# Seven 256-blocks for each 512x512 weight product, with group tiles and a new emission order

## The chip, the cores and the metric

The kernel runs on one core of a Trainium2 chip. The metric is device time in microseconds (us) of one launch. The engines are named as the profile names them: PE (TensorE, matmuls and transposes) with PEld (its weight loads), DVE (VectorE), ACT (ScalarE), POOL (GpSimd) and SP (SyncE, which issues most transfers). Each engine runs its own queue of instructions; semaphores join the queues. On PE an fp32 matmul leaves two records in the trace, each with its own weight load.

## The reference, cut to what matters

`x` is 128 x 128 x 512 (batch, node, feature) in fp32, `adj` is 128 x 128. Four layers follow one another, each with a residual and a layer norm over the 512 features:

```python
# layer 0: aggregate over nodes, then a 512x512 weight
x = _layernorm(x + (einsum('nm,bmd->bnd', adj, x) @ weight + bias))
# layer 1: scores of all pairs of nodes, masked by adj.T, scaled by their row norm, times values
q = einsum('bnd,ed->bne', x, Wq); k = einsum('bnd,ed->bne', x, Wk); v = einsum('bnd,ed->bne', x, Wv)
rel = adj.T * einsum('bnd,bmd->bnm', q, k)
x = _layernorm(x + einsum('bnm,bmd->bnd', rel / norm(rel, axis=2), v))
# layer 2: graph attention; h = x @ W; s1, s2 = h @ a1, h @ a2
att = softmax(leaky_relu(s1[:, :, None] + s2[:, None, :], 0.2) * adj, axis=2)
x = _layernorm(x + elu(att @ h + beta * h))
# layer 3: W1 = W2 = adj; the largest value over the features, then relu
A = einsum('od,bdn->bon', adj, x); C = A + b
x = _layernorm(x + max(relu(A[:, :, None, :] + (C - A)[:, :, :, None]), axis=-1))
```

## The kernel before, in words

The 128 batch elements are taken in 32 groups of four (`G = 4`, `NG = 32`). A tile of one element is 128 nodes (partitions) by 512 features. Every layer is a function that returns a list of steps for one group, and each step issues the instructions of one element or of the whole group.

**Layer 0** (`layer0`): `aggregate(b)` multiplies by `adjT` and leaves the transposed result in PSUM (p_y, L211); ACT copies it out as `yT` (L219); POOL adds the bias to `x` into `x1` (L208). `project(b)` multiplies `yT` by `w0_sb`, four matmuls of 128 x 512 (p_o, L224), and DVE adds `x1` out of PSUM (L227). `stats` (L165, L166) and `normalize` follow.

**Layer 1** (`layer1`): `turn(b)` transposes an element on PE (p_xT, L189), ACT copies it into `xT` (L190). `middle(c)` multiplies the group's `xT` by a 128-column part of `m_qk`, the product of Wq and Wk (p_t, L258), ACT copies it to `tT` (L265). `scores` gives p_rel (L271), DVE multiplies by `adj` (L279), POOL squares (L281), `norms` sums the squares on PE (p_n, L296) and a power on POOL gives the reciprocal norms. `values(b)` multiplies by `wvT` (p_v, L287; ACT copies, L291). `attend(b)` multiplies `rel` by the values (p_o, L304), DVE scales and adds the residual (L305).

**Layer 2** (`layer2`): `dots(b)` takes two products with `wa` on DVE (scr, L343, both inputs in SBUF, each with an accumulator). `logits` turns them on PE (p_s, L356), then DVE adds and takes the leaky relu (L362, L368), POOL multiplies by `adj` (L369), DVE finds the maximum (L371), ACT takes four exponentials (L374), DVE takes the reciprocal (L382) and scales (L384, with the beta term added). `turn_att` transposes the attention (p_eT, L392; ACT copies, L394), `gather(b)` multiplies `x2` by it (p_z, L399; ACT copies, L407), `project(b)` multiplies by `w2_sb` (p_h, L412). The elu is one exponential on ACT from PSUM (L416) and two operations on DVE (L417, L420).

**Layer 3** (`layer3`): `widen(b)` multiplies by `adjT` (p_a, L449), DVE finds the row maximum (L451) and adds the bias (L453), ACT adds it to the tile (L454); at the end four output transfers are issued from SP (L460).

`normalize` adds epsilon on DVE (L174), takes the power -0.5 on POOL (L169), and then makes four passes on DVE, one for each element: subtract the mean, multiply by the reciprocal deviation (L178).

So each group has four products with a 512 x 512 weight (lines L224, L258, L287, L412), of 16 matmuls (32 records) each. All tiles of an element are their own (`tiles(...)`, ten buffers for a tag), and PSUM is one pool of eight banks.

The order of the work is that in which the steps are called. Each step of layer `l` of group `g` has a place, and the steps are called in the order of their places:

```python
for g in range(NG):
    for l, layer in enumerate((layer0, layer1, layer2, layer3)):
        steps = layer(g)
        for i, f in enumerate(steps):
            pieces.append((g + 1.15 * l + (i + 0.5) / len(steps), l, f))
```

So in one unit of place layer 0 of a group, layer 1 of the group before, layer 2 of the one before that, and so on, are interleaved. Two pieces of set-up have places of their own: `prepare_weights` (`m_qk`, `wvT`) at 1.0 and `prepare_scores` (`wa`, eight DVE products in L120 and eight transposes) at 1.5. The framework derives the semaphores from the tiles, and sets the final order within each engine's queue itself.

## Time and profile before

| | |
|---|---|
| time, median of 3 runs (lowest, highest) | 2537.17 us (2536.48, 2537.85) |
| the profiled execution's own time | 2536.99 us |
| its span in the profile | 2535.2 us |
| matmuls of one 512x512 product | 1024 records, 458 to 461 us busy |
| matmuls of 128 columns: p_y, p_z, p_rel | 136.4, 138.0, 119.6 us busy |
| p_a and p_o of `attend` (512 columns) | 134.0 and 131.0 us busy |
| DVE: BATCH_NORM_STATS2 (L165) | 512 of 685 ns |
| DVE: norm passes (L178) | 512 of 540 ns, 243.9 us |
| DVE: addition out of PSUM (L227) | 128 of 683 ns |
| DVE: `dots` (L343) | 256 of 681 ns |
| ACT: copy out of PSUM (L265) | 128 of 586 ns |
| ACT: pass with a bias for each partition (L454) | 128 of 722 ns |
| POOL: bias addition (L208) | 128 of 1370 ns (median 1272) |
| POOL: power of 128x4 (L169) | 128 of 1043 ns |
| load of x for one group | 1024 KB, 5.7 us to landing |
| granted clock of PE, mean | 0.994 |

The busy time of an engine is the time in which at least one of its instructions ran; a mean duration on PE is longer than the distance between two matmuls, since they are pipelined, so distances are taken from the starts in the timeline. The span is cut in 40 slices in the page; PE is at nine tenths or more in all but the first and the last.

### The profile page before, as it was taken

To read this page: it belongs to the slowest core of one execution; us is meant where nothing else is said; L and a number is where in the kernel's file an instruction comes from. 1 tells how busy PE (TensorE), PEld (TensorE's weight loads), DVE (VectorE), ACT (ScalarE), POOL (GpSimd) and SP (SyncE) were. 2 spreads that over 40 slices of the span, in tenths; PEclk is the share of its full clock that TensorE was granted. 3 is DMA by queue.
4 is the path that set the end of the run, shared out by engine and by line. 5 is a ranking of instruction groups with operands and counts; after the bars stand their busy time and mean duration, and the time that the engine had idled before them with its cause. 6 is when DMAs were issued, how large, how long until landed. Compare 5 with 4: busy or idle time off the path is not lost.

```text
span 2535.2 us, 23625 instructions
## 1 busy us (share of the span) xinstructions
PE 2467.0 (97%) x8761; PEld 1338.9 (53%) x8761; DVE 1373.8 (54%) x3287; ACT 597.1 (24%) x1192; POOL 414.3 (16%) x358
## 2 busy tenths in 40 slices
PE   7999999999999999999999999999999999999994
PEld 4555555555555555555555555555555555555552
DVE  3354555554556655555645555545566455555466
ACT  1122222222222222222222222222222222222222
POOL 2111111111111111111211111111111111111011
PEclk9999999999999999999999999999999999999997
DMA  4000000000000000000000000000000000000001
GB/s 146 17 17 17 34 34 29 22 17 34 34 34 17 34 17 34 34 33 17 17 34 34 34 22 29 17 34 34 34 17 31 19 34 34 34 17 1 17 17 50
DMA packets 38802, 74.71 MB, mean 29 GB/s; under 512 B 2976, under 2 KB 3104, under 8 KB 38688
## 3 DMA queue, kind: packets, MB, share of 16 engines
q1 hardware_dynamic: 36960, 69.81, 7.5%
q10 hardware_dynamic: 1728, 3.41, 0.4%
q8 instruction: 69, 1.13, 0.2%
q14 instruction: 45, 0.37, 0.0%
HBM read 39.65 MB, written 33.55 MB: 29 GB/s over the span
## 4 chain that ended last, share of the span: by engine, by line
PE 96%; DVE 2%; ACT 2%; DMA 0%; POOL 0%; issue 0%; POOLq 0%; DVEq 0%; SPq 0%; ACTq 0%
PE p_t L258 18%; PE p_o L224 17%; PE p_v L287 17%; PE p_h L412 17%; PE p_z L399 5%; PE p_y L211 5%; PE p_rel L271 5%; PE p_o L304 4%; PE p_a L449 4%; PE p_xT L189 2%; ACT xT L190 1%; PE p_n L296 1%; PE p_eT L392 1%; PE p_m L142 1%; PE p_s L356 1%; DVE x L178 0%
## 5 line engine op out<-in xcount | busy, mean ns | idle before, releaser
L258 PE MATMUL p_t<-xT,m_qk 128*128 128x512 f32 x1024 | 458.2, 595 | 23.4 <-ACT xT L190 23.4
L224 PE MATMUL p_o<-w_sb,yT 128*128 128x512 f32 x1024 | 460.6, 593 | 0.0
L412 PE MATMUL p_h<-w_sb,zT 128*128 128x512 f32 x1024 | 460.6, 592 | 0.0
L287 PE MATMUL p_v<-wvT,xT 128*128 128x512 f32 x1024 | 460.5, 592 | 0.0
L227 DVE TENSOR_TENSOR x<-p_o,x 128x512 f32<-128x512 f32 x128 | 87.4, 683 | 558.3 <-PE p_o L224 558.3
L165 DVE BATCH_NORM_STATS2 st<-x 128x6 f32<-128x512 f32 x512 | 343.1, 685 | 34.6 <-ACT x L454 29.9
L258 PEld LDWEIGHTS p_t<-xT,m_qk 128*128 128x128 f32 x1024 | 189.5, 190 | 245.8 <-issue 214.5
L412 PEld LDWEIGHTS p_h<-w_sb,zT 128*128 128x128 f32 x1024 | 189.6, 190 | 214.3 <-issue 206.9
L178 DVE TENSOR_SCALAR x<-x,mv,rstd 128x512 f32<-128x512 f32 x512 | 243.9, 540 | 96.3 <-POOL rstd L169 96.3
L224 PEld LDWEIGHTS p_o<-w_sb,yT 128*128 128x128 f32 x1024 | 187.5, 191 | 199.5 <-issue 199.5
L287 PEld LDWEIGHTS p_v<-wvT,xT 128*128 128x128 f32 x1024 | 187.3, 190 | 199.4 <-issue 199.2
L208 POOL TENSOR_TENSOR x<-x,bias_sb 128x512 f32<-128x512 f32 x128 | 175.0, 1370 | 459.9 <-DVE x L305 440.5
L169 POOL TENSOR_TENSOR rstd<-ve,mhalf 128x4 f32<-128x4 f32 x128 | 132.5, 1043 | 633.5 <-DVE ve L174 621.2
L265 ACT COPY tT<-p_t 128x512 f32<-128x512 f32 x128 | 75.1, 586 | 499.3 <-PE p_t L258 499.3
L417 DVE SCALAR_TENSOR_TENSOR x<-p_h,x 128x512 f32<-128x512 f32 x128 | 88.0, 688 | 163.9 <-ACT m L416 163.9
L343 DVE SCALAR_TENSOR_TENSOR scr<-x,wa 128x512 f32<-128x512 f32 x256 | 174.4, 681 | 1.2
L211 PEld LDWEIGHTS p_y<-adjT,x 128*128 128x128 f32 x1024 | 135.6, 194 | 67.6 <-issue 67.3
L291 ACT COPY v<-p_v 128x512 f32<-128x512 f32 x128 | 74.3, 581 | 398.9 <-PE p_v L287 398.9
L399 PEld LDWEIGHTS p_z<-eT,x 128*128 128x128 f32 x1024 | 132.7, 193 | 46.5 <-issue 31.8
L416 ACT ACTIVATE m<-p_h 128x512 f32<-128x512 f32 x128 | 76.4, 597 | 330.2 <-PE p_h L412 327.3
L449 PE MATMUL p_a<-x,adjT 128*128 128x512 f32 x256 | 134.0, 608 | 14.1 <-DVE x L178 14.1
L211 PE MATMUL p_y<-adjT,x 128*128 128x128 f32 x1024 | 136.4, 277 | 8.0 <-DMA x<-in_x_dram 8.0
(62 smaller groups left out, 1979.8 us busy)
## 6 DMA issues: line engine op xcount, KB each, us to landing
x<-in_x_dram SPq DMA_DIRECT2D x32, 1024.0 KB, 5.7
out_dram<-x SPq DMA_DIRECT2D x128, 256.0 KB, 2.5
w_sb<-in_L_gnn_weight_dram ACTq DMA_DIRECT2D x1, 1024.0 KB, 5.9
wq_sb<-in_L_gnn_Wq_dram SPq DMA_DIRECT2D x1, 1024.0 KB, 16.1
wk_sb<-in_L_gnn_Wk_dram ACTq DMA_DIRECT2D x1, 1024.0 KB, 12.5
wv_sb<-in_L_gnn_Wv_dram SPq DMA_DIRECT2D x1, 1024.0 KB, 19.2
w_sb<-in_L_gnn_W_dram ACTq DMA_DIRECT2D x1, 1024.0 KB, 17.5
a_sb<-in_L_gnn_a_dram SPq DMA_DIRECT2D x1, 512.0 KB, 16.1
```

The source lines that it names most:

```text
L165: nc.vector.bn_stats(st, t)
L169: nc.gpsimd.tensor_tensor(r, v, mhalf, ALU.pow)
L178: nc.vector.tensor_scalar(ts[b], ts[b], mv[:, b, 0:1], r[:, b : b + 1], op0=ALU.subtract, op1=ALU.mult)
L208: nc.gpsimd.tensor_tensor(x1[g][b], xb, bias_sb, ALU.add)
L211: nc.tensor.matmul(p[:, k * P : (k + 1) * P], xb[:, k * P : (k + 1) * P], adjT, start=True, stop=True,)
L224: nc.tensor.matmul(p, yT[b][:, k, :], w0_sb[:, k, :], start=(k == 0), stop=(k == K - 1))
L258: nc.tensor.matmul(p, m_qk[:, k, c * P : (c + 1) * P], s["xT"][:, k, :, :].rearrange("p b n -> p (b n)"), start=(k == 0), stop=(k == K - 1),)
L287: nc.tensor.matmul(p, s["xT"][:, k, b, :], wvT[:, k, :], start=(k == 0), stop=(k == K - 1))
L343: nc.vector.scalar_tensor_tensor(scr, x2[g][b], 1.0, wa[:, i, :], op0=ALU.mult, op1=ALU.mult, accum_out=s["s"][:, i, b : b + 1],)
L399: nc.tensor.matmul(p[:, k * P : (k + 1) * P], x2[g][b][:, k * P : (k + 1) * P], s["eT"][:, b, :], start=True, stop=True,)
L412: nc.tensor.matmul(p, s["zT", b][:, k, :], w2_sb[:, k, :], start=(k == 0), stop=(k == K - 1))
L449: nc.tensor.matmul(p, adjT, x3[g][b], start=True, stop=True)
```

## The change

**The products.** The product of the group's 512 x 512 left factor (four elements of 128 nodes) with a 512 x 512 weight is cut into halves on both sides and formed from seven products of 256-blocks instead of eight (the Winograd form of Strassen's scheme). The weight sides (`weight_blocks`, four DVE operations for a weight) are made once, in set-up. The left sides are made for each product of each group (`left_factors`, four POOL operations). Each of the seven is four matmuls of 256 columns. Partial sums are kept in PSUM: blocks 1, 6, 7 and 4 add up in one region, 5 and 3 in a second one, 2 has a third; between the blocks the region's present state is taken out, by ACT as a copy where it is the first term of its quarter of the result, by DVE as an addition otherwise (in layer 0 always by DVE, onto `x1`).

```diff
+    ORDER = (1, 5, 2, 6, 3, 7, 4)
+    def left_factors(aT, tag, name, keep):
+        def blk(nh, kh):
+            return aT[:, 2 * kh : 2 * kh + 2, 2 * P * nh : 2 * P * (nh + 1)]
+        sums = work.tile([P, 3 + keep, 2, 2 * P], FP, tag=tag, name=f"s_{name}")
+        s1, s2, s4 = (sums[:, i] for i in range(3))
+        s3 = sums[:, 3] if keep else blk(1, 0)
+        nc.gpsimd.tensor_tensor(s1, blk(1, 0), blk(1, 1), ALU.add)
+        nc.gpsimd.tensor_tensor(s2, s1, blk(0, 0), ALU.subtract)
+        nc.gpsimd.tensor_tensor(s3, blk(0, 0), blk(1, 0), ALU.subtract)
+        nc.gpsimd.tensor_tensor(s4, blk(0, 1), s2, ALU.subtract)
+        return {1: blk(0, 0), 2: blk(0, 1), 3: s4, 4: blk(1, 1), 5: s1, 6: s2, 7: s3}
+    def by_rows(p, a, b, first):
+        for j in range(2):
+            for k in range(2):
+                nc.tensor.matmul(
+                    p[:, j, :],
+                    a[:, k, j * P : (j + 1) * P],
+                    b[:, k, :],
+                    start=(first and j == 0 and k == 0),
+                    stop=(j == 1 and k == 1),
+                    skip_group_check=True,
+                )
...
+        def put(dst, p):
+            if after is None:
+                nc.scalar.copy(dst, p)
+            else:
+                nc.vector.tensor_tensor(dst, p, dst, ALU.add)
+        def add(dst, p):
+            nc.vector.tensor_tensor(dst, p, dst, ALU.add)
+        def step(i):
+            a, b = factors()[i], weights()[i]
+            where = {1: 0, 6: 0, 7: 0, 4: 0, 2: 1, 5: 2, 3: 2}[i]
+            first = i in (1, 2, 5)
+            mul(region(where) if first else r[where], a, b, first)
+            p = r[where]
+            if i == 1:
+                put(c(0, 0), p)
+            elif i == 5:
+                put(c(1, 1), p)
+            elif i == 2:
+                add(c(0, 0), p)
+            elif i == 6:
+                put(c(0, 1), p)
+            elif i == 3:
+                add(c(0, 1), p)
+            elif i == 7:
+                add(c(1, 1), p)
+            else:
+                put(c(1, 0), p)
```

The weight sides:

```diff
+        t2, t3, t4 = t[:, 0], t[:, 1], t[:, 2]
+        nc.vector.tensor_tensor(t3, blk(1, 1), blk(0, 1), ALU.subtract)
+        nc.vector.tensor_tensor(t2, t3, blk(0, 0), ALU.add)
+        nc.vector.tensor_tensor(t4, blk(1, 0), t2, ALU.subtract)
+        nc.vector.tensor_tensor(blk(0, 1), blk(0, 1), blk(0, 0), ALU.subtract)
```

**Tiles and PSUM.** `x1`, `x2`, `x3`, the values and the layer-2 result are one tile for a group ([128, 4, 512]); `x` is loaded straight into `x1`, and POOL adds the bias in place after the aggregation has read it. PSUM is two pools of tags with four banks each: `ps` for single results, `r` for the regions of the products.

**The elu** is a step of its own (`elu(b)`): the layer-2 result is first copied or added into SBUF (`s["c"]`), and the exponential and the two DVE operations read it there.

**The norm passes** move to ACT, with one more small DVE operation for a group:

```diff
+        nm = small.tile([P, G], FP, tag="nmean", name=f"nmean_{key[0]}_{key[1]}")
+        nc.vector.scalar_tensor_tensor(nm, mv[:, :, 0], -1.0, r, op0=ALU.mult, op1=ALU.mult)
         for b in range(G):
-            nc.vector.tensor_scalar(
-                ts[b], ts[b], mv[:, b, 0:1], r[:, b : b + 1], op0=ALU.subtract, op1=ALU.mult
+            nc.scalar.activation(
+                t[:, b, :], t[:, b, :], AF.Identity, bias=nm[:, b : b + 1], scale=r[:, b : b + 1]
             )
```

**The order.** Each part of a layer is given a stretch of places of its own (`emit((from, to), *steps)`), with `t` = g - 1, g, g + 1 and g + 2 in layers 0, 1, 2 and 3, which follow one another here:

```diff
+        emit((t + 0.0, t + 0.2), *each(aggregate))
+        emit((t + 0.2, t + 0.21), sums)
+        emit(
+            (t + 0.25, t + 0.5),
+            *product(
+                f"y_{g}", by_rows, lambda: s["f"], lambda: bw["0"], rows_of(lambda: x1[g]), after
+            ),
+        )
+        emit((t + 0.5, t + 0.51), lambda: normalize((0, g), x1[g]))
...
+        emit((t - 0.2, t - 0.05), *each(turn))
+        emit((t - 0.05, t - 0.04), sums)
+        emit(
+            (t + 0.0, t + 0.25),
+            *product(
+                f"m_{g}", by_columns, lambda: s["f"], lambda: bw["m"], middle_block, None
+            ),
+        )
+        emit((t + 0.28, t + 0.46), *each(scores))
+        emit((t + 0.5, t + 0.51), norms)
+        emit(
+            (t + 0.5, t + 0.75),
+            *product(
+                f"v_{g}", by_rows, lambda: s["f"], lambda: bw["v"], rows_of(lambda: s["v"]), None
+            ),
+        )
+        emit((t + 0.76, t + 0.97), *each(attend))
+        emit((t + 0.98, t + 0.99), end)
...
+        emit((t + 0.0, t + 0.1), *each(dots))
+        emit((t + 0.1, t + 0.11), logits)
+        emit((t + 0.25, t + 0.26), turn_att)
+        emit((t + 0.29, t + 0.47), *each(gather))
+        emit((t + 0.5, t + 0.51), sums)
+        emit(
+            (t + 0.75, t + 1.0),
+            *product(
+                f"z_{g}", by_rows, lambda: s["f"], lambda: bw["2"], rows_of(lambda: s["c"]), None
+            ),
+        )
+        emit((t + 0.93, t + 1.05), *each(elu))
+        emit((t + 1.06, t + 1.07), end)
...
+        emit((t + 0.52, t + 0.74), *each(widen))
+        emit((t + 0.78, t + 0.79), end)
...
+    emit((-0.6, -0.59), prepare_qk)
+    emit((-0.1, -0.09), prepare_v)
+    emit((0.45, 0.46), prepare_scores)
```

In what follows Y, M, V and Z are the four products (layer 0, `m_qk`, values, layer 2), M5 is block 5 of M, and y0, at0, w0, xT0, elu0 are the steps of the group's first element; sumsY, sumsX and sumsZ are the left sides. M and V share sumsX. From one M to the next, the order of the places is: M1, y0, M5, y1, M2, `logits`, M6, y2, M3, y3, M7, sumsY, M4, `turn_att`, Y1, rel0, Y5, z0, Y2, rel1, z1, Y6, rel2, z2, Y3, rel3, Y7, z3, Y4, sumsZ, `norms`, norm of layer 0, V1, w0, V5, V2, w1, V6, w2, V3, V7, w3, V4, Z1, norm of layer 3, at0, Z5, xT0, at1, Z2, xT1, Z6, at2, xT2, Z3, xT3, at3, elu0, Z7, sumsX, elu1, Z4, norm of layer 1, elu2; dots0 to dots3, elu3 and the norm of layer 2 stand among M1 to M2.

## The prediction

> **What bounds the kernel now.** I read the page's busy shares first, then its chain of work that ended last, then the rows of the costliest lines, and last the timeline.
>
> ```profile
> PE 2467.0 (97%) x8761; PEld 1338.9 (53%) x8761; DVE 1373.8 (54%) x3287; ACT 597.1 (24%) x1192; POOL 414.3 (16%) x358
> ...
> PE 96%; DVE 2%; ACT 2%; DMA 0%; POOL 0%; issue 0%; POOLq 0%; DVEq 0%; SPq 0%; ACTq 0%
> ...
> L258 PE MATMUL p_t<-xT,m_qk 128*128 128x512 f32 x1024 | 458.2, 595 | 23.4 <-ACT xT L190 23.4
> L224 PE MATMUL p_o<-w_sb,yT 128*128 128x512 f32 x1024 | 460.6, 593 | 0.0
> ```
>
> TensorE is busy 97% and owns 96% of the chain: only less work on it, or less waiting, can shorten the span. Each fp32 matmul leaves two records, so a product of a group is 16 matmuls and 32 records. The timeline repeats every 77.03 us (the first `p_t` of two groups starts at 1263.44 and 1340.47), and 32 x 77.03 = 2465 of 2535.2 us; 70 us are start and end.
>
> ```profile
> 1209.30 1.05 PE L211 MATMUL p_y<-adjT,x 128*128 128x128 f32 x8
> 1210.19 3.74 PE L271 MATMUL p_rel<-tT,xT 128*128 128x128 f32 x32
> 1213.76 3.60 PE L287 MATMUL p_v<-wvT,xT 128*128 128x512 f32 x8
> 1217.20 0.60 PE L392 MATMUL p_eT<-ident,e 128*128 128x128 f32 x4
> ...
> 1261.67 1.04 PE L189 MATMUL p_xT<-ident,x 128*128 128x128 f32 x8
> 1263.44 3.70 PE L258 MATMUL p_t<-xT,m_qk 128*128 128x512 f32 x8 [0.73 <-ACT xT L190]
> ```
>
> From start to start: 32 records of 128 columns take 3.57 us (0.1116 each), 8 of 512 take 3.44 (0.430; 0.4294 over longer runs). The last row is a hand-over, TensorE to ScalarE and back: 0.59 us of copy cost 0.73 of idle after the matmul's modelled end, about 0.9 after its last column. It is the one wait of a group.
>
> **1. Work removed from TensorE.** A group's four products are 128 records of 0.4294 = 54.96 us. All else in the period is 77.03 - 0.73 - 54.96 = 21.34. Afterwards a product is 7 blocks of 8 records with 256 columns, 224 in all. No row has 256 columns: half a 512 gives 0.2147, two of 128 give 0.223; the straight line between both gives 0.217, which I take. 224 x 0.217 = 48.6 (48.1 to 50.0). A period without any wait is then **69.95 us**, 7.1 less.
>
> **2. Work added elsewhere, per group.** VectorE loses 16 norm passes (243.9/32 = 7.6 us) and gains 12 additions out of PSUM at 0.683 (8.2) and 4 small products (0.7): 43 us become 44. ScalarE gets the norm passes (16 x 0.72, by its nearest row, L454) and 4 copies: 18.7 become about 33. GpSimd gets 16 block sums at 1.27 (the adds of L208 and L369): 12.9 become 33. None of them fills 70 us; the question is when they are needed. The Trainium skill (ScalarE: Activation LUTs, section What ACT_TABLE_LOAD costs) adds some 93 ns for each pointer operand, and the new pass has two: about 0.8 us a pass, 1.3 us more a group on an engine half idle, which moves nothing. In set-up the four weights' block sums (16 adds of 0.68) run while inputs land or other set-up goes on.
>
> **3. New waits inside a product.** The order is 1, 5, 2, 6, 3, 7, 4, and 1, 6, 7, 4 add up in one PSUM region, each after the previous eviction. Step 4 comes directly after 7: eviction 0.68 plus hand-over, 0.9 to 1.1, less what is written between. In M nothing stands between (**1.1**); in Y a gather of 0.89 (**0.2**); in V a `widen` matmul of 0.86 (**0.4**); in Z only VectorE work (in step 4). Other reuses have two blocks or more between, 1.7 us and up, against an eviction of 0.6.
>
> **4. The wait that decides: `logits`.** TensorE runs as written. In the last group it waited 5.94 us for `e` though the `p_a` behind it was ready, and ran that only afterwards:
>
> ```profile
> 2484.01 0.48 PE L356 MATMUL p_s<-ident,s 128*128 128x128 f32 x1 [1.09 <-DVE scr L343]
> ...
> 2490.43 1.17 PE L392 MATMUL p_eT<-ident,e 128*128 128x128 f32 x4 [5.94 <-DVE e L384]
> 2491.39 1.92 PE L449 MATMUL p_a<-x,adjT 128*128 128x512 f32 x2
> ```
>
> VectorE, by contrast, takes what is ready: the set-up products of L120, written last, run ahead of the first evictions. The new places give, around a period's end, for TensorE: at3, Z7, Z4, M1, y0, M5, y1, M2, then the four transposes of `logits`, which need all `dots`. The `dots` need the layer-1 norm, which needs at3. From the end of at3 TensorE has 4 + 1 blocks at 1.74 and 2 x 0.89 (y): 5 x 1.74 + 1.78 = 10.5 us until it stands at `logits`. VectorE meanwhile has, back to back at 0.61 an operation: at3 1.4, the rest of elu0 1.3, Z7's eviction 0.6, elu1 1.9, elu2 1.9, elu3 1.9, eight `dots` 5.4, two norms' small steps 0.6, together **15.1**. In the order as written the layer-1 norm stood at 5.12 and `logits` at 5.58 of a group's count, 0.46 apart; now at 4.985 and 5.105, 0.12 apart, with one group's elu and two norms in the same stretch. Without any gap TensorE loses 15.1 + 0.4 - 10.5 = 5.0, Z4's wait included: the lower bound.
>
> It is raised by GpSimd. Its rows are the two-tensor adds of L208, VectorE's the two-tensor products of L120:
>
> ```profile
> 25.09 0.69 DVE L120 SCALAR_TENSOR_TENSOR scr_wa<-w_sb,a_sb 128x512 f32<-128x512 f32 x1
> 25.83 1.64 DVE L120 SCALAR_TENSOR_TENSOR scr_wa<-w_sb,a_sb 128x512 f32<-128x512 f32 x1
> 27.50 1.63 DVE L120 SCALAR_TENSOR_TENSOR scr_wa<-w_sb,a_sb 128x512 f32<-128x512 f32 x1
> ...
> 25.62 9.23 POOL L208 TENSOR_TENSOR x<-x,bias_sb 128x512 f32<-128x512 f32 x6 [8.32 <-DMA x<-in_x_dram]
> ```
>
> While GpSimd streams, the same product takes 1.64 instead of 0.69, about one slowed product for each add, and an add 1.54 instead of 1.23 (4.93 for the four at the start). In the 15 us at issue GpSimd now has sumsX (4 x 1.27), two norm powers (1.02) and two bias adds: 9.7 us, where VectorE has 15 operations with both inputs in SBUF (elu 7, dots 8; 9.2 us). Also, sumsX is written before the layer-1 norm, whose power queues behind it: the transposed copy ends 0.2 before at3 does, sumsX 5.1 to 6.7 after it, the power at 7.9, the mean at 8.3, the first pass on ScalarE at 9.2. Then follow at least eight dots (5.4), elu3 (1.9) and the rest of elu2 (1): 17.5, and with the bias adds in between about **19**. So 19 - 10.5 = **8.5** for Z4 and `logits` together. Counted another way, by the rows above: if half of the eight GpSimd operations meet a product, 15.5 + 4 x 0.95 = 19.3, so 8.8; if all do, 23.1, so 12.6, the upper bound. I stay at 8.5, nearer the middle, since the row shows the collision but not how often it falls here.
>
> The Trainium skill (SBUF — State Buffer, section Who interferes with whom) goes further than the row: a VectorE operation with two SBUF inputs and a GpSimd operation that reads SBUF exclude each other for the whole instruction, whatever their size. By it 9.7 + 9.2 = 18.9 us would have to pass one after the other, and the wait would be at least 8.4.
>
> **5. The granted clock.** After 5.08 us of idle, the eight `p_a` at 2518.20 (eight records) took 5.40 us where eight such records take 3.60. A wait of this length each group costs **1.8** more; none if it stays short (0.73 us cost nothing).
>
> **6. What is covered.** After `logits`, softmax takes 6.8 us to the end of L384 in the period shown (1206.0 to 1212.8); TensorE has 5 blocks and two aggregates, 10 us, before `turn`, so nothing; if GpSimd's y2, y3 adds delay it by over 3 us, the rest shows at `turn`. sumsY needs 5.1 us and its first result before Y5, some 7 us later. The 0.73 wait falls away, since block M1 reads only early columns. The x load moves nothing: three x1 buffers, one period of lead, 5.7 us of landing; output DMAs leave as before.
>
> **The sum.** Waits per period: 8.5 + 1.8 + 1.1 + 0.2 + 0.4 = 12.0. Ends: 70, plus an estimated 18, as the last group has no other group's matmuls over sumsZ (5.1), its three elu operations on two late tiles (4) and the longer dots chain (9): 88. 32 x 69.95 + 88 + 31 x 12.0 = 2238 + 88 + 372 = 2698 of span. The profiled run took 2536.99 with a span of 2535.2, so 1.8 on top: **2700 us**; that run lies 0.2 below the shown median, which moves nothing.
>
> **Rivals.**
> A. **VectorE keeps up** (faster). `logits` finds its dots done, or TensorE takes other matmuls first. For it: VectorE is idle 40% of a period. Against: the 5.94 us above. With 3 us of waits: 2326 + 93 + 2 = 2421.
> B. **No collisions with GpSimd.** Waits 5.0 + 1.0 + 0.2 + 0.2 = 6.4, no slow clock: 2326 + 198 + 2 = 2526, almost the old time; what the products save the waits take. For it: in steady state the rows of L343 stay at 669 to 694 ns. Against: GpSimd had 13 us a group there, not 33. It turns from gain to loss at 6.75 us of waits.
> C. **Worse blocking.** An order on VectorE that sets a norm's step, which waits for GpSimd, ahead of ready work. For it: 0.89 us of VectorE idle before the norm at 2479.61, with a `dots` product still to come. Against: it fills other gaps. The upper bound of step 4 with the clock's 1.8 and 2.6 for the products: 12.6 + 1.8 + 2.6 = 17.0, 2326 + 527 + 2 = 2855.
> D. **256-column matmuls not at half price**: at 0.223 each the main sum rises by 45, to 2745. Within the range.
>
> **Chances.** Forecast (2580 to 2800, D within it) 0.52; A 0.20; B 0.17; C 0.11. A measurement can tell about 0.2% (5 us) from no change. Faster: A and half of B, 0.28; same 0.03; slower 0.69. The range reaches down to 2430, which keeps B and the upper part of A, and up to 2820; about 0.2 is left out. The forecast's own range is 2580 to 2800.
>
> **What would show it.** Records of 256 columns 0.217 apart; `p_s` idle before it of 4 to 8 us in each group, released by `scr`; Z's and M's step 4 each waiting for VectorE; dots with mean over 0.9 us; TensorE's clock below 0.99 in the middle slices. Wrong would be: TensorE still at 97%, idle before `p_s` under 1 us, or `dots` at 0.68.

## The result, and the profile after

The changed kernel takes **2743.08 us** (median of four runs, 2735.86 to 2756.68) against 2537.09 us for the kernel before: 1.0818 times as long (95% interval 1.0776 to 1.0861). The prediction was 2700 us, 43 less; the measured time lies inside its range of 2430 to 2820 and inside the forecast's own range of 2580 to 2800. The profiled run is the shortest of the four, 2735.86 us with a span of 2734.1.

The page of the changed kernel, busy times and the chain that ended last by engine:

```profile
PE 2415.9 (88%) x11833; PEld 1984.9 (73%) x11833; DVE 1599.0 (58%) x3299; ACT 1021.5 (37%) x1836; POOL 923.2 (34%) x742
...
PEclk8999999999999999999999999999999999999997
...
PE 45%; POOL 20%; DVE 16%; ACT 14%; issue 4%; DMA 1%; ACTq 0%; POOLq 0%; DVEq 0%
```

TensorE's share fell from 97 to 88%, and it owns 45% of the chain instead of 96%: the end is now set by work that passes between four engines. GpSimd, at 34% busy, has the second largest share of the chain. Its 384 additional instructions (742 instead of 358) are twelve block sums a group; the prediction had counted sixteen.

TensorE's waits by releaser: us in all, times, longest:

```profile
PE p_s L474 <- ACT m L538: 92.1, 30, 3.1
PE p_eT L510 <- DVE e L502: 76.3, 62, 5.9
PE p_s L474 <- DVE scr L461: 45.8, 39, 5.8
PE r_v L212 <- DVE v L250: 30.8, 29, 1.1
PE r_z L212 <- DVE c L250: 14.4, 32, 2.1
```

The first row and the third are one wait, that of the transposes of `logits` for the `dots`. An exponential of the elu ended at about the time of the first wait's end, so the view names it; the product that the transpose reads (a `scr` row) ended at 1360.80 + 0.08, just ahead of the matmul at 1361.03.

One period in TensorE's timeline (start, duration, and in brackets the idle time before and what ended it):

```profile
1350.71 1.99 PE L212 MATMUL r_z<-t,zT 128*128 128x256 f32 x8 [0.37 <-DVE c L250]
...
1361.03 0.45 PE L474 MATMUL p_s<-ident,s 128*128 128x128 f32 x1 [3.09 <-ACT m L538]
1361.27 3.47 PE L225 MATMUL r_m<-s_x,t_m 128*128 128x256 f32 x8
...
1368.93 0.32 PE L474 MATMUL p_s<-ident,s 128*128 128x128 f32 x1 [0.90 <-DVE scr L461]
...
1376.96 0.33 PE L510 MATMUL p_eT<-ident,e 128*128 128x128 f32 x1 [1.40 <-DVE e L502]
1378.23 0.73 PE L510 MATMUL p_eT<-ident,e 128*128 128x128 f32 x2 [0.94 <-DVE e L502]
...
1396.06 0.83 PE L404 MATMUL p_n<-ones,sq 128*128 128x1 f32 x6 [0.36 <-POOL sq L398]
1414.03 1.99 PE L212 MATMUL r_v<-t_v,xT 128*128 128x256 f32 x8 [1.06 <-DVE v L250]
```

The `p_s` after the first wait returns at 1444.00, so this period is **82.97 us** (77.03 before); 28 of them, from 207.93 to 2531.79, have a mean of 83.0. Its idle stretches add up to 0.37 + 3.09 + 0.90 + 1.40 + 0.94 + 0.36 + 1.06 = 8.12, within 0.02 of the period less TensorE's busy 74.83 in it. The block of M behind the long wait takes 3.31 us to the next start where a block takes 1.73. The granted clock shows both places; windows of 5 us, with each engine's busy time and, after POOL's, the clock:

```profile
1361.03:1366.00 4.97, 4.97 (x20) 4.28 (x21) 4.91 (x16) 1.28 (x4) 0.17 (x1) 0.66 0.00 0
1366.00:1371.00 5.00, 4.10 (x24) 3.53 (x23) 2.89 (x7) 3.06 (x5) 3.29 (x3) 1.00 0.00 0
...
1376.00:1381.00 5.00, 3.10 (x13) 2.83 (x14) 3.30 (x5) 0.58 (x1) 2.03 (x2) 0.71 0.00 0
```

0.34 of 4.97 us and 0.29 of 5.00 are 3.1 us lost to the clock, and 0.3 more in the next window, with 0.95: 3.4 us. (The window from 1441.00 to the next long wait's end shows 0.82, but TensorE is idle in it, so nothing is lost there.) So 69.95 (TensorE's work as predicted) + 8.1 + 3.4 = 81.5. Idle times understate the rest: a block's modelled end lies 0.16 us behind the start of its successor, and seven such places give 1.1. The last 0.4 us are not traced.

What made `p_s` late is the chain of the changed kernel (start, us, what), from the last transposed copy of x to that transpose:

```profile
1346.07 0.59 ACT xT L370
1346.66 0.07 issue
1346.73 1.53 POOL s_x L202
1348.25 1.68 POOL s_x L204
1349.93 1.24 POOL s_x L203
...
1351.24 1.59 POOL s_x L205
...
1352.93 1.40 POOL rstd L291
...
1354.36 1.24 DVE nmean L300
...
1355.62 0.81 ACT x L302
```

Four block sums of x for the next product stand on GpSimd ahead of the power that the layer-1 norm of another group needs. VectorE's small operations of the norm are slow as well: `ve` (the variance plus epsilon, which the power reads) ran 1.23 us from 1351.63, beside the last sum, and the mean 1.24 us, beside a bias addition, both at 128 x 4 elements. The sums end at 1352.83 and `ve` at 1352.86, so the power was held up by both.

### The profile page after: what moved, and what is told of

The parts are those of the page before. It is cut to its first block, busy times and chain, and to the rows that moved or that the text cites. A ratio compares the mean times of both kernels' runs of the same rounds, so it can differ in the third digit from the quotient of the medians.

```text
span 2734.1 us, 30874 instructions
## 1 busy us (share of the span) xinstructions
PE 2415.9 (88%) x11833; PEld 1984.9 (73%) x11833; DVE 1599.0 (58%) x3299; ACT 1021.5 (37%) x1836; POOL 923.2 (34%) x742
## 4 chain that ended last, share of the span: by engine, by line
PE 45%; POOL 20%; DVE 16%; ACT 14%; issue 4%; DMA 1%; ACTq 0%; POOLq 0%; DVEq 0%
PE r_y L212 10%; PE r_z L212 10%; ACT x L302 6%; PE p_rel L386 5%; PE p_z L519 4%; PE r_m L225 4%; POOL rstd L291 4%; PE r_v L212 3%; PE p_o L415 3%; DVE st L287 3%; ACT x L576 2%; PE p_xT L367 2%; ACT e L492 2%; POOL s_x L204 2%; DVE nmean L300 2%
## 5 line engine op out<-in xcount | busy, mean ns | idle before, releaser
L302 ACT ACTIVATE x<-x,nmean,rstd 128x512 f32<-128x512 f32 x512 | 381.5, 805 | 355.0 <-DVE nmean L300 355.0
L247 DVE TENSOR_TENSOR x<-r_y,x 128x512 f32<-128x512 f32 x128 | 88.0, 688 | 285.2 <-PE r_y L212 285.2
L526 ACT COPY zT<-p_z 128x512 f32<-128x512 f32 x128 | 74.9, 585 | 421.3 <-PE p_z L519 421.3
L416 DVE SCALAR_TENSOR_TENSOR x<-p_o,rn,x 128x512 f32<-128x512 f32 x128 | 95.9, 749 | 132.5 <-PE p_o L415 132.5
L225 PE MATMUL r_m<-s_x,t_m 128*128 128x256 f32 x512 | 165.1, 480 | 0.0
L576 ACT ACTIVATE x<-x,top 128x512 f32<-128x512 f32 x128 | 91.8, 718 | 169.9 <-DVE top L575 168.3
L386 PE MATMUL p_rel<-tT,xT 128*128 128x128 f32 x1024 | 153.5, 293 | 0.0
L386 PEld LDWEIGHTS p_rel<-tT,xT 128*128 128x128 f32 x1024 | 149.4, 210 | 4.9
L250 DVE TENSOR_TENSOR x<-r_y,x 128x512 f32<-128x512 f32 x96 | 65.2, 680 | 146.3 <-PE r_y L212 146.3
L212 PE MATMUL r_y<-w_sb,s_y 128*128 128x256 f32 x512 | 143.6, 419 | 2.0 <-POOL s_y L202 2.0
L519 PE MATMUL p_z<-eT,x 128*128 128x128 f32 x1024 | 137.6, 279 | 0.7 <-ACT eT L512 0.7
```

Of the source, the lines that this page charges most:

```text
L212: nc.tensor.matmul(p[:, j, :], a[:, k, j * P : (j + 1) * P], b[:, k, :], start=(first and j == 0 and k == 0), stop=(j == 1 and k == 1), sk ...
L225: nc.tensor.matmul(p[:, c, :], b[:, k, c * P : (c + 1) * P], a[:, k, :], start=(first and c == 0 and k == 0), stop=(c == 1 and k == 1), sk ...
L302: nc.scalar.activation(t[:, b, :], t[:, b, :], AF.Identity, bias=nm[:, b : b + 1], scale=r[:, b : b + 1])
L386: nc.tensor.matmul(p[:, b * P : (b + 1) * P], s["xT"][:, k, b * P : (b + 1) * P], s["tT"][:, k, b * P : (b + 1) * P], start=(k == 0), stop ...
L519: nc.tensor.matmul(p[:, k * P : (k + 1) * P], x2[g][:, b, k * P : (k + 1) * P], s["eT"][:, b, :], start=True, stop=True,)
L576: nc.scalar.activation(x, x, AF.Identity, bias=top)
```

## The experiments

The kernel before took 2537.1 to 2537.7 us beside each of these. Where one value is given, it is of a single run. "The changed kernel" is put at its profiled 2735.9, the run that the traces describe.

**1. No block sums.** The left factors are plain blocks, so the result of every weight product is another one.

```diff
-        nc.gpsimd.tensor_tensor(s1, blk(1, 0), blk(1, 1), ALU.add)
...
-        return {1: blk(0, 0), 2: blk(0, 1), 3: s4, 4: blk(1, 1), 5: s1, 6: s2, 7: s3}
+        return {1: blk(0, 0), 2: blk(0, 1), 3: blk(0, 1), 4: blk(1, 1), 5: blk(1, 0), 6: blk(1, 1), 7: blk(1, 0)}
```

> Leaves out the 16 left-side block sums of a group on GpSimd: each of the seven blocks reads a plain block of the left factor, so the products are not the reference's; matmuls, evictions and order stay. Theory S (the stretch: TensorE waits at logits and turn because elu, dots and norms follow one another on VectorE, lengthened by collisions with GpSimd's sums, and each long wait lowers the clock): the waits at p_s and p_eT fall from 6.4 us a group to 2 to 3, e at L502 goes back to about 350 ns, and the period from 83 us to 75 to 78, so 2490 to 2590 us. Rival P (the blocks themselves: PSUM regions taken out between dependent blocks, 256-column matmuls): no change, 2720 to 2760. Rival N (the norm passes on ScalarE): no change beyond 1%.

Measured: **2529.0 us**. The sums cost 207 us, though TensorE does exactly the same matmuls. (GpSimd loses 12 sums a group, not 16.) The first line of its page and TensorE's waits in this run, by its own line numbers:

```profile
PE 2328.9 (92%) x11833; PEld 1929.5 (76%) x11833; DVE 1477.7 (58%) x3299; ACT 1024.6 (41%) x1836; POOL 441.4 (17%) x358
```

```profile
PE p_s L467 <- DVE scr L454: 113.4, 96, 5.8
PE p_eT L503 <- DVE e L495: 16.8, 21, 5.9
...
PE r_v L205 <- DVE v L243: 7.1, 29, 0.2
```

TensorE is idle 198 us instead of 318: 60 less at `p_eT`, 24 less at `p_s`, 24 less at V's block 4. The other 87 us are the same matmuls in less time (2328.9 busy instead of 2415.9), at a mean granted clock of 0.984 instead of 0.953. The two waits that theory S names come to 4.1 us a group, not the 2 to 3 that it gave: most of the wait at `p_s` stays without the sums.

**2. Logits later.**

```diff
-        emit((t + 0.1, t + 0.11), logits)
-        emit((t + 0.25, t + 0.26), turn_att)
-        emit((t + 0.29, t + 0.47), *each(gather))
-        emit((t + 0.5, t + 0.51), sums)
+        emit((t + 0.27, t + 0.28), logits)
+        emit((t + 0.47, t + 0.48), turn_att)
+        emit((t + 0.5, t + 0.66), *each(gather))
+        emit((t + 0.68, t + 0.69), sums)
```

> Order only: logits from place 0.10 to 0.27, turn_att from 0.25 to 0.47, gather from 0.29-0.47 to 0.50-0.66, sumsZ from 0.50 to 0.68. Theory S: the waits at p_s and p_eT and the slow clock after them go; the period becomes 71.5 to 75 us, 2380 to 2490 us, below the kernel before. Rival P: 2700 to 2750, since no product changes. Rival N: little, 2680 to 2750, as the norm passes stay on ScalarE.

Measured: **2594.8 us**. The `p_s` wait is almost gone (11.6 us), but the gain is too small by over 100 us, because a new wait stands in its place. TensorE's waits and its timeline in this run:

```profile
PE r_m L225 <- DVE tT L250: 142.4, 29, 4.9
...
PE p_s L474 <- DVE scr L461: 11.6, 6, 4.7
```

```profile
1306.57 3.78 PE L225 MATMUL r_m<-xT,t_m 128*128 128x256 f32 x8 [4.91 <-DVE tT L250]
1310.14 1.13 PE L212 MATMUL r_y<-w_sb,yT 128*128 128x256 f32 x3
```

M's block 4 writes into a region that VectorE must first read after block 7, and that addition is queued behind the dots. The slow block behind the wait is there again, 3.57 us.

**3. Norm passes back on VectorE.**

```diff
-            nc.scalar.activation(
-                t[:, b, :], t[:, b, :], AF.Identity, bias=nm[:, b : b + 1], scale=r[:, b : b + 1]
-            )
+            nc.vector.tensor_scalar(
+                t[:, b, :], t[:, b, :], mv[:, b, 0:1], r[:, b : b + 1], op0=ALU.subtract, op1=ALU.mult
+            )
```

> Undoes one part: the four norm passes of each layer go back to VectorE (540 ns each, 8.6 us a group). Theory S: VectorE gets more work in the very stretch, 2740 to 2830 us. Rival N: the chain of each norm gets shorter by ScalarE's 805 ns passes and its queue, 2600 to 2700 us. Rival P: no change.

Measured: **2837.0 us**, just above theory S's range, with 302.5 us of `p_s` waits. So this part of the change helps, by about 100 us.

**4. Plain products in the new arrangement.** Sixteen matmuls of 512 columns and four evictions for each product, no block sums; tiles, order, elu and norm passes as changed.

```diff
+        def step(i):
+            a, w = factors(), weights()
+            p = psum.tile([P, D], FP, tag="r", name=f"r{i}_{name}")
+            for k in range(K):
+                if mul is by_rows:
+                    nc.tensor.matmul(
+                        p, a[:, k, i * P : (i + 1) * P], w[:, k, :], start=(k == 0), stop=(k == K - 1)
+                    )
...
-        return [lambda i=i: step(i) for i in ORDER]
+        return [lambda i=i: step(i) for i in range(G)]
```

> Keeps the new tiles, order, elu and norm passes, but makes each product as before, 16 matmuls of 512 columns with four evictions, without block sums. TensorE then has 76.3 us of work a group. Theory S: no GpSimd sums, but the stretch stays: 2 to 4 us of waits a group at p_s and p_eT, 2570 to 2660 us, slower than the kernel before although its products are the same. Rival P: the loss lies in the blocks, so 2500 to 2550. Rival N: 2570 and more, with waits for ScalarE's norm pass.

Measured: **2624.5 us**, `p_s` waiting 87.4. The arrangement alone (order, tiles, elu and norm passes together; which of them, this run doesn't show) costs 87 us; the seven blocks with their sums then add 111 more in it, where TensorE has 7.1 us a group less to do.

**5. Another order of the blocks**, with a block between 6 and 7 and one between 7 and 4. Here the first element's elu reads the layer-2 result before block 3 is added.

```diff
-    ORDER = (1, 5, 2, 6, 3, 7, 4)
+    ORDER = (1, 5, 6, 2, 7, 3, 4)
```

> One size of the products alone: the blocks in the order 1, 5, 6, 2, 7, 3, 4, so that one other block stands between any two that use the same PSUM region. Theory S: of the 13 us that a group loses, only the waits at step 4 (r_v 1.0, r_z 0.5) go, and what TensorE arrives earlier it waits longer at p_s: 2690 to 2735 us. Rival P: the reuse of the regions is the loss, 2450 to 2600.

Measured: **2717.9 us**, 18 us less, which is within the 21 us over which the four runs of the changed kernel spread. V's block 4 no longer waits for VectorE, but `p_eT` waits 107.5 us instead of 76.3. So the waits inside the products are a small part at most.

**6 and 7. Everything of layer 2 later, with the old and the new order of blocks** (the latter with the elu as in the fifth). The tile of the values is allocated in `scores` instead of `norms` here, since `norms` now comes after V's first block.

```diff
-        emit((t + 0.0, t + 0.1), *each(dots))
-        emit((t + 0.1, t + 0.11), logits)
-        emit((t + 0.25, t + 0.26), turn_att)
-        emit((t + 0.29, t + 0.47), *each(gather))
-        emit((t + 0.5, t + 0.51), sums)
+        emit((t + 0.18, t + 0.42), *each(dots))
+        emit((t + 0.46, t + 0.47), logits)
+        emit((t + 0.62, t + 0.63), turn_att)
+        emit((t + 0.63, t + 0.74), *each(gather))
+        emit((t + 0.745, t + 0.75), sums)
...
-        emit((t + 0.5, t + 0.51), norms)
+        emit((t + 0.56, t + 0.57), norms)
```

> Order only, wider than late_logits: dots from 0.00-0.10 to 0.18-0.42, logits to 0.46, turn_att to 0.62, gather to 0.63-0.74, sumsZ to 0.745, norms from 0.50 to 0.56; blocks in the order of the change. late_logits left one wait of 4.9 us, M4 for M7's addition, which stands on VectorE behind the dots. Theory S: with the dots out of the way that wait falls under 1.5 us, the clock stays at 0.98 or more, the period is 71.5 to 74 us, 2370 to 2460 us. If instead the wait only moves to the next consumer of VectorE's work, 2500 to 2590.

> Both: the places of spread and the block order 1, 5, 6, 2, 7, 3, 4. Theory S: on top of spread the waits at step 4 (0.4 to 1 us in each of M, V and Z) go: 1 to 2.5 us less a group, 2330 to 2420 us, and the period within 2 us of the 69.95 that TensorE's work alone takes.

Measured: **2631.6** and **2602.1 us**. Both missed all that was stated. In the sixth, M's block 4 waits for VectorE 161 us in all, 5.5 at most. In the seventh, the wait goes to ScalarE; its timeline, and TensorE's below it:

```profile
1371.22 2.93 ACT L302 ACTIVATE x<-x,nmean,rstd 128x512 f32<-128x512 f32 x4 [3.53 <-DVE nmean L300]
1374.05 0.61 ACT L538 ACTIVATE m<-c 128x512 f32<-128x512 f32 x1
1374.57 0.56 ACT L245 COPY tT<-r_m 128x512 f32<-128x512 f32 x1
```

```profile
1375.28 1.96 PE L225 MATMUL r_m<-s_x,t_m 128*128 128x256 f32 x8 [2.97 <-ACT tT L245]
```

The copy out of M's region stands behind four norm passes in ScalarE's queue, and ScalarE was idle 3.53 us for their mean. That both misses have one cause, places set by what `logits` needs while the late norm stayed where it was, is argued here; the ninth and tenth test it.

**8. GpSimd as busy, reading nothing.** Each block sum becomes a sum of four columns and three memsets, so the left factors are others.

```diff
+        def fill(dst, a, b):
+            nc.gpsimd.tensor_tensor(dst[:, :, :4], a[:, :, :4], b[:, :, :4], ALU.add)
+            for _ in range(3):
+                nc.gpsimd.memset(dst, 0.5)
```

> Each of the four block sums on GpSimd is replaced by a sum of 4 columns (so that it still waits for its inputs) and three fills of the whole block with a constant, which read nothing; the left factors are then not the reference's. GpSimd is busy about as long as before. Theory C (collisions: two-input VectorE operations and GpSimd instructions that read SBUF get in each other's way): e at L502 goes back to 350 ns, and the time falls most of the way to that of no_sums, 2530 to 2620. Theory Q (the queue on GpSimd alone, the norm's power behind the sums): the time stays within 2680 to 2760.

Measured: **2696.9 us**, GpSimd busy 1080 us (923 in the changed kernel). VectorE's softmax operation (L502 of the changed kernel) takes 348 ns again instead of 808, and the waits at `p_eT` fall from 76 to 47 us; `p_s` still waits 155. So the slowing of VectorE beside GpSimd's sums accounts for at least some 40 of the 207 us; the rest stays as long as GpSimd is occupied in the same places, which points to its queue. The split is rough: GpSimd is 17% busier here, and TensorE's wait for it at `p_n` rises from 11 to 43 us.

**9. Sums of x earlier.** Only the place of x's transposes and sums changes.

```diff
-        emit((t - 0.2, t - 0.05), *each(turn))
-        emit((t - 0.05, t - 0.04), sums)
+        emit((t - 0.24, t - 0.13), *each(turn))
+        emit((t - 0.125, t - 0.12), sums)
```

> Only the order changes: the transposes of x and GpSimd's sums of x are issued earlier (transposes from -0.24 to -0.13 of a group's place instead of -0.2 to -0.05, the sums at -0.125 instead of -0.05), so that the four sums run before the layer-1 norm's small operations instead of beside them. Theory L (the late end of the layer-1 norm makes the dots late and so the logits' transposes wait; in the changed kernel the sums of x stood at 1346.73 to 1352.8 us, ve took 1.23 us beside them and the power came at 1352.93): the norm ends 2 to 3 us earlier and the p_s wait falls from 4.3 us per group to about 2: 2640 to 2700 us. Rival B (the dots end late because VectorE works through eight of them with the ELU's operations between, whatever the norm does): p_s keeps its 4 us, 2720 to 2755 us.

Measured: **2639.5 us** (two runs; 1.0403 of before, 1.0373 to 1.0433), 96 us below the changed kernel. The time is at the edge of what theory L said, but its row is not: `p_s` waits 133.8 us in all, hardly less. Counted from the start of the last residual addition of layer 1 (L416), the mean now comes after 5.6 us instead of 7.3 and the last dot ends after 20.1 instead of 21.8. What fell is another wait, `p_eT` with 36.5 instead of 76.3 us, and the time that the same matmuls take: TensorE is busy 2365.0 us instead of 2415.9, at a mean granted clock of 0.972 instead of 0.953. The wait at `p_s` is in three pieces (1.28, 0.64 and 2.20 us). In one group of three the block behind the last piece isn't slow, in the other two it takes 2.4 to 3.4 us to the next start instead of 1.73; two groups that follow one another:

```profile
1334.79 0.32 PE L474 MATMUL p_s<-ident,s 128*128 128x128 f32 x1 [2.20 <-DVE scr L461]
1334.95 1.89 PE L225 MATMUL r_m<-s_x,t_m 128*128 128x256 f32 x8
...
1414.24 0.32 PE L474 MATMUL p_s<-ident,s 128*128 128x128 f32 x1 [2.20 <-DVE scr L461]
1414.40 2.92 PE L225 MATMUL r_m<-s_x,t_m 128*128 128x256 f32 x8
```

VectorE's timeline in this run shows what is left:

```profile
1332.90 1.22 DVE L300 SCALAR_TENSOR_TENSOR nmean<-mv,rstd 128x4 f32<-128x4 f32 x1 [0.90 <-POOL rstd L291]
1334.05 0.68 DVE L461 SCALAR_TENSOR_TENSOR scr<-x,wa 128x512 f32<-128x512 f32 x1
```

The mean of another norm (layer 2's) stands ahead of the last dot, waits 0.90 us for GpSimd, and takes 1.22 us beside a bias addition.

**10. Early sums and later logits together**: the edit of the ninth, and

```diff
-        emit((t + 0.1, t + 0.11), logits)
-        emit((t + 0.25, t + 0.26), turn_att)
-        emit((t + 0.29, t + 0.47), *each(gather))
-        emit((t + 0.5, t + 0.51), sums)
+        emit((t + 0.2, t + 0.21), logits)
+        emit((t + 0.4, t + 0.41), turn_att)
+        emit((t + 0.44, t + 0.6), *each(gather))
+        emit((t + 0.61, t + 0.62), sums)
```

> The order of the kernel with early sums of x, and besides the logits at 0.2 instead of 0.1, the turn of the attention matrix at 0.4, the gather from 0.44 to 0.6 and the sums of z at 0.61. Theory L: the p_s wait goes, and because the dots end earlier than in the kernel that only had the late logits (there 2594.8 us with 4.9 us a group at M4, whose input waited for an addition behind the dots) M4's wait is 2 us or less: 2450 to 2540 us. Rival B (VectorE's queue holds dots, ELU and the M additions in one stretch, so the wait at M4 stays): 2570 to 2620 us.

Measured: **2524.4 us** (three runs, 2523.2 to 2525.9): 0.995 of the kernel before (0.9927 to 0.9973), **the one full version that beats both**, the kernel before by 0.5%. TensorE's timeline in it:

```profile
1268.13 0.32 PE L474 MATMUL p_s<-ident,s 128*128 128x128 f32 x1 [2.25 <-DVE scr L461]
...
1269.93 3.78 PE L225 MATMUL r_m<-xT,t_m 128*128 128x256 f32 x8 [1.04 <-DVE tT L250]
1273.50 2.73 PE L212 MATMUL r_y<-w_sb,yT 128*128 128x256 f32 x6
```

M's block 4 waits 1.04 instead of 4.91 us, as theory L has it; `p_s` keeps 2.25, which it did not say.

**11. The sums on VectorE.**

```diff
-        nc.gpsimd.tensor_tensor(s1, blk(1, 0), blk(1, 1), ALU.add)
+        nc.vector.tensor_tensor(s1, blk(1, 0), blk(1, 1), ALU.add)
```

and the same for the three others.

> The sixteen block sums of a group go from GpSimd to VectorE, nothing else (there are twelve in a group: four each for y, x and z). VectorE's additions of this size take 0.68 us where they don't meet GpSimd, so 12 x 0.68 = 8.2 us a group more on VectorE, and the lengthening beside GpSimd (about 6 us a group) goes. Theory S (the sums cost what they do through GpSimd: its queue and the slowed VectorE): near the kernel without sums (2529 us), plus what 8 us of VectorE in its queue delay: 2540 to 2650 us. Rival V (any work added to VectorE delays the dots, as with the norm passes on VectorE, which gave 2837 us with 8 to 9 us a group more): 2720 to 2850 us.

Measured: **2607.0 us** (two runs; 1.0275, 1.0245 to 1.0304). VectorE is busy 1754 us, 155 more, and the kernel is 129 us faster than with the sums on GpSimd. VectorE's row of the softmax operation in this run, and in the changed kernel after it:

```profile
L502 DVE SCALAR_TENSOR_TENSOR e<-e,rs,beta_i 128x128 f32<-128x128 f32 x128 | 36.2, 345 | 0.1
```

```profile
L502 DVE SCALAR_TENSOR_TENSOR e<-e,rs,beta_i 128x128 f32<-128x128 f32 x128 | 96.1, 808 | 1.1
```

So it isn't any work added to VectorE that hurts: 4.8 us more a group there cost less than the sums do on GpSimd.

**12. The tenth's order, moved further.** M's blocks spread over a longer stretch with a block of Y between 7 and 4, and logits at 0.255.

```diff
-            (t + 0.0, t + 0.25),
+            (t + 0.0, t + 0.34),
             *product(
                 f"m_{g}", by_columns, lambda: s["f"], lambda: bw["m"], middle_block, None
...
-        emit((t + 0.28, t + 0.46), *each(scores))
+        emit((t + 0.36, t + 0.48), *each(scores))
...
-            (t + 0.25, t + 0.5),
+            (t + 0.22, t + 0.5),
             *product(
                 f"y_{g}", by_rows, lambda: s["f"], lambda: bw["0"], rows_of(lambda: x1[g]), after
```

> The order of the kernel with early sums of x and late logits, moved a little further, so that neither the logits' transposes (2.25 us of waiting in its profiled group, 77 us in the run) nor M4 (1.0 us, 30 us in the run, and then eight records at 3.78 instead of 1.73 us) is the next thing TensorE has: logits at 0.255, turn 0.43, gather 0.47 to 0.62, sums of z 0.63; M's seven blocks spread over 0.0 to 0.34, Y's over 0.22 to 0.5, so that a block of Y stands between M7 and M4; scores from 0.36. Theory L (the loss of the change is waits of TensorE on VectorE and GpSimd that the order makes, and the half clock behind them; with them gone the seven blocks' gain shows): 2524 less about 32 x (2.25 + 1.04 + 2.0) = 170 us, 2340 to 2440 us, faster than the kernel before. Rival B (VectorE's and ScalarE's queues are so full that any order moves the wait to the next consumer, as with the three other orders): 2490 to 2560 us.

Measured: **2546.9 us** (five runs; 1.0038, 1.0024 to 1.0052), slower than the tenth. M's block 4 no longer waits, and `p_s` waits more (121 us in all instead of 77). VectorE's and then GpSimd's timeline in this run:

```profile
1280.60 1.65 DVE L461 SCALAR_TENSOR_TENSOR scr<-x,wa 128x512 f32<-128x512 f32 x1
1282.17 0.08 DVE L461 DVE_READ_ACCUMULATOR scr<-x,wa 128x1 f32 x1
...
1284.45 1.22 DVE L300 SCALAR_TENSOR_TENSOR nmean<-mv,rstd 128x4 f32<-128x4 f32 x1 [0.90 <-POOL rstd L291]
1285.59 0.68 DVE L461 SCALAR_TENSOR_TENSOR scr<-x,wa 128x512 f32<-128x512 f32 x1
```

```profile
1279.98 1.71 POOL L202 TENSOR_TENSOR s_y<-yT 128x512 f32<-128x512 f32 x1
...
1283.02 1.39 POOL L291 TENSOR_TENSOR rstd<-ve,mhalf 128x4 f32<-128x4 f32 x1 [1.33 <-DVE ve L296]
```

All four aggregations now run ahead of `p_s`, so the sums of y begin before the dots are done and run beside them: the dots' mean is 878 ns (731 in the tenth, 675 in the changed kernel). The last dot again stands behind the mean that waits for GpSimd's power, and `p_s` waits 0.58 + 3.10 us. The time is in rival B's range, and as rival B has it the wait has moved.

## Why the prediction was right, point by point

**The sum.** Predicted were 69.95 us of work and 12.0 of waits and slow clock a group; measured are 82.97, so 13.0. The total is right within a twelfth, and partly by luck, since errors of opposite sign cancel: the wait at `logits` is 4.1 us smaller than its term, while the turn of the attention, which had no term, takes 2.3 and the clock 1.6 more than was put down. With 31 times 13.05 us of waits (by the mean period of 83.0) the ends come out at 91 us (88 predicted).

**Work on TensorE: right.** Eight records of 256 columns stand 1.73 us apart, 0.216 each; 0.217 was taken. Rival D is out.

**Added work elsewhere: fits, as said, but mis-sized.** GpSimd has 923 us / 32 = 28.9 a group; 33 were predicted, four sums too many. ScalarE has 31.9 (about 33 predicted), a norm pass takes 805 ns. VectorE has 50.0 instead of 44 with the work that was counted: 3.8 of the 6 us go when the sums are left out (1477.7 us busy in experiment 1), and the rest isn't traced in full; without the sums `ve` still takes 407 ns and the elu's second operation 801, as GpSimd's other operations stay. The Trainium skill (ScalarE: Activation LUTs, section What ACT_TABLE_LOAD costs) charges some 93 ns for each pointer operand, which agrees with 805 ns for two pointers beside 718 for the pass with one.

**Waits inside a product: small, as predicted, but not where.** V's block 4 waits 1.06 (0.4 predicted), M's and Y's not at all (1.1 and 0.2): 1.06 together where 1.7 were put down. Ahead of M's block 4 half a block of Y ran, and VectorE had ended its dots at 1368.9; where `logits` goes later, M's wait comes out at 4.9.

**The wait at `logits`: the mechanism right, a premise false, the size half.** 8.5 us were predicted for Z's block 4 and `logits`; they are 0.37 + 3.99 = 4.4. The dots were predicted to end 19 us after the last `attend` step ends on TensorE (1346.9); the last one ends at 1368.9, 22 us. But "TensorE runs as written" does not hold, though the description of the kernel says that the framework sets the final order: the final order on TensorE took block 1 of M ahead of Z's block 4, and put blocks of M and aggregations between the four transposes, so most of the 22 us are filled. The chain that the prediction built, block sums, power, mean, norm pass, dots, is the one that the profile shows, and experiments 1, 9 and 10 act on it: taking the sums away gives 207 us, moving x's transposes and sums ahead of the norm 96, and with the logits later 212. But the sums' part in this one wait was overrated: without them `p_s` still waits 113 of 138 us, 3.5 us a group, where the prediction's bound without any collision was 5.0 with Z's block 4 included. Most of what experiments 1 and 9 win lies at the turn of the attention and in the clock.

**What is covered: wrong.** The prediction put nothing at the turn of the attention; 2.34 us wait there each group (76.3 us in all). The softmax's last step takes 4 x 808 ns beside the sums of y instead of 4 x 347. The prediction's "if GpSimd's y2, y3 adds delay it by over 3 us" was thought of for GpSimd's queue; the cost came in good part by the slowed VectorE. Experiments 8 and 11 bring the operation back to 348 and 345 ns. It isn't the whole of the wait: `p_eT` still waits 46.6 us in experiment 8 and 28.2 in experiment 11.

**The clock: right in kind, half in size.** 1.8 us were predicted; 3.4 were lost, since the two waits at the turn of the attention have a slow stretch of their own (0.71).

**Where the collisions fall: wrong.** "Dots with mean over 0.9 us" was given as a sign, and dots at 0.68 as a sign of being wrong. They stayed at 675 ns, because GpSimd's sums of x are over (1352.83) when the dots begin (1358.64). The sums slow other operations: L502, the elu's first (880 ns; 744 without the sums) and in part `ve` (511 ns; 407 without the sums, 166 in experiment 10). The elu's second operation, 781 ns, isn't their doing: it takes 801 without them, and 680 with the sums on VectorE. By the Trainium skill (SBUF — State Buffer, section Who interferes with whom) a VectorE operation with two SBUF inputs and a GpSimd operation that reads SBUF exclude each other; the rows agree where the two meet, for L502 and even for the mean of 128 x 4 elements, and memsets, which read nothing, left L502 at 348 ns. `ve`, which reads a single tile, was slowed too. By its sum the dots were to end after 18.9 us and the wait was to be 8.4 at least; they ended after 22, and the wait was still only 4.4, because TensorE had other matmuls to run meanwhile.

**Rivals.** A's time (2421) is out, but its second condition, that TensorE takes other matmuls first, came partly true, and with it the wait is half of its term. B (no collisions) is out for this kernel; its 2526 us are close to experiment 1, where there are no sums (2529.0). C was partly there: layer 2's mean, with the last dot behind it, stands on VectorE for 2.17 us (to 1368.11), while GpSimd makes a bias addition and then the power. (Two slips that move nothing: the prediction's list of VectorE's work adds up to 15.0 and not 15.1, and VectorE is idle 45% of a period of the kernel before, 42.43 of 77.03 us busy, not 40%.)

**So where did the gain go?** The seven blocks take 7.1 x 32 = 227 us off TensorE. The new arrangement without the blocks costs 87 (experiment 4), and the sums on GpSimd 207 (experiment 1); measured in different kernels, the two need not add up. With order and sums settled better (experiment 10) 13 us of gain remain. Open is whether more can be had: the sums on VectorE were not tried with the tenth's order, and a norm without GpSimd's power wasn't tried at all.

## What to carry to other kernels

When a bottleneck engine is relieved by giving a helper engine more work, look at what that helper already does for others: GpSimd was busy only a third of the time, but the added sums stood ahead of a 1 us power at the head of a long chain, and slowed VectorE's operations beside them. Moving a consumer later cures its wait only if the producers' queue has nothing else that is due in the same stretch; first move the work that delays the producer, then the consumer (96 us from the first move, 115 more from the second). A sum of waits can be right in total and wrong in place, so check each term against its row before acting on it.

## What was not expected of the hardware

- **The clock gives way after short idle, but not each time.** The 5.08 us known from before is not needed: after 3.09 us of idle the next eight records took 3.31 us instead of 1.73, and after two stretches of 1.40 and 0.94 us close together the granted clock was 0.71 over 5 us. In experiment 10, 2.25 and 1.04 us close together had the same effect (3.57 us for eight records); 0.73 us alone, in the kernel before, had not. The length of the idle alone doesn't decide. In the changed kernel the same 3.09 or 3.10 us left the next block at 1.80 us in three groups (at 372.30, 618.02 and 863.76), and in experiment 9 one group of three stays at 1.73. What decides between them isn't shown. The first of the three:

```profile
372.30 0.29 PE L474 MATMUL p_s<-ident,s 128*128 128x128 f32 x1 [3.09 <-ACT m L538]
372.43 1.96 PE L225 MATMUL r_m<-s_x,t_m 128*128 128x256 f32 x8
```

- **Tiny operations can be held up for a whole addition.** A VectorE operation of 128 x 4 elements takes 0.16 us alone and up to 1.24 beside a GpSimd addition: `ve` ended at 1352.86 where the sum beside it ended at 1352.83, the mean at 1355.59 where the bias addition ended at 1355.56.
- **GpSimd's additions are slowed too, and differently by place.** The sums of x took 1.53, 1.72, 1.26 and 1.59 us in the period shown, those of y, at the same size, 1.26 to 1.31.
